# Four layers on one core: one copy per block end in layer 0, layer 1's norms in parts with its gates between the projections, and layer 2's norm in four parts

## The chip, the cores and the metric

The kernel runs on one core of one Trainium2 chip, in one launch. The metric is the device time of that core in microseconds (us); lower is better. A core has five engines with instruction queues of their own: PE (matrix products), ACT (activation functions, copies), DVE (elementwise work and statistics), POOL (elementwise work) and SP, which here only issues DMA transfers. Each takes its instructions in the order in which they were written into its queue, and waits where an operand isn't ready or a buffer isn't free.

## What is computed

The input `x` has the shape [2, 64, 64, 128] (batch, height, width, channels), all in fp32. Four layers are added to it in turn:

```python
x = x + L0_conv(_gn(x))      # attention over 4096 positions, 4 heads, relative-position bias
x = x + L1_conv(_gn(x))      # gated product, below
t = x as [2, 4096, 128]
t = t + L2_attn(_ln_t(t))    # causal, silu(scores**2), plus a positional product
t = t + L2_ffn(_ln_t(t))     # 64 experts, each takes its 8 best tokens
t = t + L3_attn(_ln_t(t))    # softmax attention over 4096 positions
t = t + L3_ffn(_ln_t(t))     # 8 experts, top 2 of a token
```

`_gn` is a group norm (32 groups), `_ln_t` a layer norm over the channels. The second layer, in which most of the change lies:

```python
xn = layer_norm(x, norm_a, norm_b)
left = (xn @ Wl + bl) * sigmoid(xn @ Wlg + blg)
right = (xn @ Wr + br) * sigmoid(xn @ Wrg + brg)
out_gate = sigmoid(xn @ Wog + bog)
out = einsum("bkjd,bkid->bijd", left, right) / n
out = layer_norm(out, on_a, on_b) * out_gate
return out @ Wo + bo
```

## The kernel before

`x` stays in SBUF as 64 rows of 128x128 (32 rows a batch; a "block" is four rows, 512 positions). Layers follow one another; where the text of one layer issues work of the next, it is interleaved by hand.

**Layer 0** (`l0_bounded`, L464). A unit is a batch, a pair of heads and a half of the queries: 8 units. Each has four query blocks of 512, and each block goes over 32 key tiles `k`: 1024 iterations and 32 block ends. An iteration makes scores (`sc`, PE, L588), exp (ACT, L596, into `es`), and a multiply by the bias `ew` (DVE, L597). `values()` (L538) runs two iterations behind: eight passes on PE (L546) add to the PSUM tile `o`, which has one buffer. With the last `k` of a block it copies `o` to `os`, half on ACT (L555), half on DVE (L556), since the value passes of the next block need `o`. `l0_finish` (L699) then adds the two halves (L705), transposes, divides and adds to `x`. Side work (the next unit's operands, statistics for layer 1, and layer 1's input norm for batch 0) is a list of generators, of which `piece()` and `more()` take steps in certain iterations.

**Layer 1** (`layer1`, L841). The input norm of batch 1 is `l1_rows` (L406): group norm of eight blocks on DVE (`group_norm`, two operations each, L157 and L158), statistics of all 32 rows (`row_stats`: bn_stats L165 and bn_aggr L166 for each row), one reciprocal root (`rstd`, L88: seven small steps with a square root on ACT and one Newton step), and then the norm of the rows, odd ones on ACT (L428), even ones on DVE (L169). `l1_turn` (L436) transposes a block on PE and scales it on ACT (L444). `gates(b, g)` makes the output gate's projection of a block: PE (L897) and ACT (L900) into `gate`; the gates of batch 0 stand before the norm, those of batch 1 between the turns. The projection loop goes over j = 0, 2, ... 62: two products of 128x512 into a PSUM tile, bias on DVE, sigmoid on ACT, two multiplies on POOL. Every fourth iteration takes the sigmoid of a part of `gate` (L947). The product stage makes `tri` (512 small products on PE, 16 ACT copies); the 16 additions of the bias `bo` to `x` (L974) are written there, but depend on nothing in it and were placed earlier in DVE's queue, between the steps of the norm of batch 1. The output norm goes over four groups of 16 columns: `stats`, then for each 4 columns the norm (three on ACT, one on DVE), transposes, an ACT step with the norm's scale and bias, and a multiply by the gate on POOL (for part of the last group on DVE, L995). `next(toeplitz)` issues the loading of layer 2's positional table (`l2_table`). Last, 16 blocks of `out @ Wo` are made on PE and added to `x` on DVE.

**Layer 2** (`layer2_attn`, L1083). Its parts are generators in a dictionary `jobs`, from which a planner takes steps between the iterations of the attention according to the steps left and the iterations left (`due`); `finish(key)` runs one to its end. `norm_stats(b)` (L1185) makes the statistics of all 32 rows of a batch and one reciprocal root; `keys(b, g)` needs them, normalizes block `g` (L169) and makes keys and values. Before the first iteration `norm_stats(0)`, `keys(0, 0)` and `prepare(0, 7, 0)`, the queries of the first block to be attended (block 7), are run to their end.

**Layer 3** (`l3_bounded`, L1935). Sixteen query blocks of 16 iterations each; `piece()` takes one step of a queue of jobs in each iteration, and two in the very first block. After the second to last block the routing of batch 1 and seven bias jobs (`f3_bias`, L1919: a transpose on PE, a copy on ACT, a product on PE, an addition on DVE) are queued; what isn't done when the last block ends is done after the loop. The experts follow.

## Time and profile before

| | us |
|---|---|
| median of three runs | 4883.54 (4882.14 to 4885.44) |
| the profiled execution | 4879.15 |
| its span in the profile | 4877.3 |

The profile shows one execution. Its stages, read from the timeline (us from the start of the span):

| stage | from | to |
|---|---|---|
| layer 0, loop | 120 | 2166 |
| layer 1, end of group norm of batch 1 | 2166 | 2182.7 |
| layer 1, norm of batch 1 and turns | 2182.7 | 2235.9 |
| layer 1, projection loop | 2235.9 | 2294.5 |
| layer 1, product | 2294.5 | 2312.3 |
| layer 1, output norm | 2312.3 | 2361.3 |
| layer 1, `out @ Wo` and additions to `x` | 2361.3 | 2378.1 |
| layer 2, up to the first scores | 2378.1 | 2397.8 |
| layer 2, attention and experts | 2397.8 | about 3780 |
| layer 3, attention | about 3780 | 4737 |
| layer 3, remaining bias jobs | 4737 | 4751 |
| layer 3, experts | 4751 | 4877 |

In the profile a group of instructions is named by its line, engine, operation, and the tile it writes, then (after `<-`) the tiles it reads. A time in brackets is how long the engine had been idle before an instruction, with what released it. PEclk is the share of full clock that PE was granted in a window. A window's row gives busy microseconds of each engine, with the count of its instructions.

### The profile page before, as it was taken

The page shows a single profiled execution, that of the slowest core. Times are in us where ns is not written, and L with a number is a line of the kernel's source. Part 1 is how long each engine was busy: PE and PEld are TensorE (multiplying, and loading weights), DVE is VectorE, ACT ScalarE, POOL GpSimd, SP SyncE. Part 2 cuts the span into 40 slices and gives each one's busy share as a digit, 9 for nine tenths or more (in the row PEclk, how much of TensorE's full clock was granted, in tenths as well). Part 3 has the DMA queues.
Part 4 walks back from the last instruction along what each step waited for, and adds up shares of the span by engine and source line. Part 5 has one row for each costly group of instructions (what it writes and reads, how often), then busy time and mean ns, then how long its engine had stood idle before and what let it go on. Part 6 is the DMA issues. An engine that isn't in the chain of part 4 may idle for free.

```text
span 4877.3 us, 78242 instructions
## 1 busy us (share of the span) xinstructions
PE 4514.3 (93%) x33260; PEld 1766.5 (36%) x33260; DVE 2943.3 (60%) x4845; ACT 2647.6 (54%) x3077; POOL 943.7 (19%) x848
## 2 busy tenths in 40 slices
PE   6999999999899999987789999999986999999999
PEld 4333333333233333335322223323224444444444
DVE  4676767676766767765755656555553544454447
ACT  3655555555556555554567666676740433333326
POOL 1000000000000000003355554655530100000008
PEclk7999999999999999998799999999987999999999
DMA  1000000000000000000000000000016000000001
GB/s 46 10 1 10 1 10 1 10 1 1 10 1 10 1 12 1 1 6 15 10 1 1 1 1 1 1 1 1 1 52 232 1 0 0 1 0 1 0 1 35
DMA packets 43210, 60.29 MB, mean 12 GB/s; under 512 B 4352, under 2 KB 25056, under 8 KB 41696
## 3 DMA queue, kind: packets, MB, share of 16 engines
q1 hardware_dynamic: 41552, 54.34, 3.6%
q8 instruction: 265, 4.34, 0.4%
q10 hardware_dynamic: 1296, 0.82, 0.1%
q14 instruction: 97, 0.79, 0.1%
HBM read 42.56 MB, written 4.19 MB: 10 GB/s over the span
## 4 chain that ended last, share of the span: by engine, by line
PE 37%; DVE 6%; ACT 3%; POOL 3%; issue 2%; DMA 0%; POOLq 0%; DVEq 0%; ACTq 0%
PE scl L2047 9%; PE oTl L2006 9%; PE l2sc L1422 5%; PE l2pos L1180 4%; PE l2av L1468 3%; PE f3ex L2156 2%; DVE l2es L1442 2%; POOL l2es L1445 2%; ACT l2es L1453 1%; ACT l2es L1433 1%; PE l2po L1388 1%; DVE l2a L169 0%; PE f3fpb L1930 0%; PE pol L1975 0%; PE l2pu L1180 0%
## 5 line engine op out<-in xcount | busy, mean ns | idle before, releaser
L597 DVE TENSOR_TENSOR l0es<-l0es,l0ew 128x1024 f32<-128x1024 f32 x1024 | 1252.0, 1227 | 601.5 <-ACT l0es L596 601.5
L596 ACT ACTIVATE l0es<-l0sc 128x1024 f32<-128x1024 f32 x1024 | 1042.7, 1023 | 722.5 <-PE l0sc L588 712.8
L546 PE MATMUL l0o<-l0es,l0v 64*33 64x512 f32 x8192 | 1070.0, 592 | 51.7 <-DVE l0os L556 46.4
L588 PE MATMUL l0sc<-l0qa,ka 64*64 64x512 f32 x8192 | 1081.9, 596 | 4.6 <-ACT l0es L596 4.6
L1453 ACT ACTIVATE l2es<-l2es 128x1024 f32<-128x1024 f32 (+3 forms) x576 | 559.3, 984 | 270.1 <-POOL l2es L1445 263.0
L1445 POOL TENSOR_TENSOR l2es<-l2es 128x1024 f32<-128x1024 f32 (+3 forms) x352 | 581.1, 1661 | 494.3 <-DVE l2es L1442 439.2
L2014 DVE TENSOR_TENSOR accl<-accl,esl 128x1024 f32<-128x1024 f32 x240 | 302.6, 1261 | 425.8 <-ACT esl L2058 422.4
L1442 DVE TENSOR_SCALAR l2es<-l2sc 128x1024 f32<-128x1024 f32 (+3 forms) x320 | 338.8, 1059 | 315.1 <-PE l2sc L1422 314.8
L2058 ACT ACTIVATE esl<-scl 128x1024 f32<-128x1024 f32 x240 | 245.5, 1023 | 481.7 <-PE scl L2047 456.6
L546 PEld LDWEIGHTS l0o<-l0es,l0v 64*33 64x33 f32 x8192 | 258.0, 108 | 659.3 <-issue 564.3
L588 PEld LDWEIGHTS l0sc<-l0qa,ka 64*64 64x64 f32 x8192 | 294.7, 133 | 546.8 <-issue 480.5
L2047 PE MATMUL scl<-l3qT,l3kT 128*128 128x512 f32 x1024 | 486.8, 595 | 0.0
L1422 PE MATMUL l2sc<-l2q,kept 32*128 32x512 f32 (+3 forms) x2304 | 389.4, 619 | 88.6 <-ACT l2es L1433 65.3
L2006 PE MATMUL oTl<-esl,l3v 128*128 128x512 f32 x960 | 450.9, 592 | 0.0
L722 POOL TENSOR_TENSOR x<-x,l0y 128x256 f32<-128x256 f32 x32 | 23.4, 732 | 2074.1 <-DVE l0y L717 1945.6
L1468 PE MATMUL l2av<-l2es,kept 128*32 128x512 f32 (+3 forms) x2304 | 310.6, 589 | 0.0
L1180 PE MATMUL l2pos<-kept 128*32 128x512 f32 x2416 | 297.0, 598 | 0.0
L2047 PEld LDWEIGHTS scl<-l3qT,l3kT 128*128 128x128 f32 x1024 | 188.5, 191 | 208.2 <-issue 192.5
L2006 PEld LDWEIGHTS oTl<-esl,l3v 128*128 128x128 f32 x960 | 181.8, 190 | 225.8 <-issue 221.5
L1433 ACT ACTIVATE l2es<-l2sc 128x1024 f32<-128x1024 f32 x224 | 226.1, 1009 | 53.9 <-PE l2sc L1422 52.5
L1422 PEld LDWEIGHTS l2sc<-l2q,kept 32*128 32x128 f32 x2304 | 115.9, 186 | 331.5 <-ACT l2es L1433 166.2
L1971 POOL TENSOR_TENSOR bothl<-accl 128x512 f32<-128x512 f32 x16 | 20.2, 1263 | 633.6 <-DVE accl L2014 633.6
(690 smaller groups left out, 3825.3 us busy)
## 6 DMA issues: line engine op xcount, KB each, us to landing
f2w<-in_L_ffn_weight_dram SPq DMA_DIRECT2D x32, 1024.0 KB, 13.4
l0ew<-l0ew SPq DMA_DIRECT2D x16, 512.0 KB, 5.1
x<-in_x_dram SPq DMA_DIRECT2D x8, 512.0 KB, 9.0
out_dram<-x SPq DMA_DIRECT2D x16, 256.0 KB, 2.3
kept<-in_L_attn_pos_rev_dram SPq DMA_DIRECT2D x1, 1792.0 KB, 6.7
ew<-in_L_ffn_expert_w_dram SPq DMA_DIRECT2D x1, 512.0 KB, 4.0
kept<-in_L_attn_pos_rev_dram SPq DMA_DIRECT2D x1, 256.0 KB
f2b<-in_L_ffn_weight_dram ACTq DMA_DIRECT2D x2, 128.0 KB, 2.5
```

The lines of the kernel that those rows point to most:

```text
L546: nc.tensor.matmul(o[64 * h : 64 * h + HD + 1, r, :], lhsT=v1[rows, k, 2 * pair + h, :], rhs=es[rows, h, :], start=(k == 0), stop=(k == NC ...
L588: nc.tensor.matmul(sc[64 * c : 64 * c + 64, h, :], lhsT=ka[rows, k0 : k0 + 64], rhs=qa[rows, k // (NC // 2), qs], start=True, stop=True,)
L596: nc.scalar.activation(es, sc, AF.Exp)
L597: nc.vector.tensor_tensor(es, es, ew[:, :, qs], ALU.mult)
L1180: nc.tensor.matmul(out[part], lhsT=lhsT[:, part], rhs=rhs, start=start, stop=stop)
L1422: nc.tensor.matmul(sc[:, h2, off:], lhsT=kT[hs, k * P : (k + 1) * P], rhs=q[hs, off:], start=True, stop=True,)
L1442: nc.vector.tensor_scalar(es[:, :, lo:], sc[:, :, lo:], root, None, ALU.mult)
L1445: nc.gpsimd.tensor_tensor(part, part, part, ALU.mult)
L1453: nc.scalar.activation(es[:, :, off:], es[:, :, off:], AF.Silu)
L1468: nc.tensor.matmul(avs[i][hs, off:], lhsT=v[:, k, hs], rhs=es[h // 2][:, h % 2, off:], start=(k == 0), stop=last,)
L2006: nc.tensor.matmul(oT, lhsT=vs[b][:, k, :], rhs=es[:, i, :], start=(k == 0), stop=(k == NC - 1),)
L2047: nc.tensor.matmul(sc[:, i, :], lhsT=kTs[b][:, k * P : (k + 1) * P], rhs=qT[:, qb * 512 : (qb + 1) * 512], start=True, stop=True,)
```

## The change

Layer 0: at a block's end ACT copies all of `o` in one instruction, and DVE copies nothing; in the text `values()` stands ahead of the multiply by the bias.

Layer 1, input norm of batch 1: in three parts (blocks 0 to 2, 3 to 5, 6 and 7). The statistics of a part are taken jointly: bn_stats of each row writes the count, mean and sum of squares of the row's even and odd elements, and five operations on all rows of the part at once form mean and variance from them, instead of a bn_aggr for each row. The rows of the first two parts are normalized on ACT, those of the third half on ACT and half on DVE. The gate projections move into the projection loop, one in every second iteration, with the sigmoid taken straight from PSUM. `bo` is loaded into a buffer of the product stage, so that its additions can't be placed before it. The output norm uses the same joint statistics, over groups of 8, 16, 16, 16 and 8 columns; the blocks of `out @ Wo` are taken in the order 0, 7, 1 to 6, 8 to 15.

Layer 2: `norm_stats` of batch 0 is made in four parts of two blocks, the first for blocks 0 and 7; the other three are jobs of the first iterations.

Layer 3: in the last block of batch 1 `piece()` is called twice in an iteration.

```diff
-    def rstd(self, out, var, eps, n, pool=None):
+    def rstd(self, out, var, eps, n, pool=None, scale=1.0):
...
-        nc.vector.tensor_scalar(v, var, eps, None, ALU.add)
+        if scale == 1.0:
+            nc.vector.tensor_scalar(v, var, eps, None, ALU.add)
+        else:
+            nc.vector.tensor_scalar(v, var, scale, eps, ALU.mult, ALU.add)
...
-                    nc.scalar.copy(os[rows, 0, :], o[rows, 0, :])
-                    nc.vector.tensor_copy(os[rows, 1, :], o[rows, 1, :])
+                    nc.scalar.copy(os[rows], o[rows])
...
-                        nc.vector.tensor_tensor(es, es, ew[:, :, qs], ALU.mult)
                         if len(waiting) == 2:
                             values()
+                        nc.vector.tensor_tensor(es, es, ew[:, :, qs], ALU.mult)
...
-            bo = self.load(wp, "bo", [P, C], row_bcast(ins["L1_conv_bo"], C))
 
             def stats(src, tag):
 
-                mv = sp.tile([P, GN, 2], F32, tag="mv", name=f"l1mv{tag}")
-                self.row_stats(mv, src, f"l1{tag}")
-                r = sp.tile([P, GN], F32, tag="r", name=f"l1r{tag}")
-                self.rstd(r, mv[:, :, 1], 1e-5, GN, sp)
-                m = sp.tile([P, GN], F32, tag="m", name=f"l1m{tag}")
-                nc.vector.scalar_tensor_tensor(m, mv[:, :, 0], -1.0, r, ALU.mult, ALU.mult)
-                return mv, r, m
+                n = src.shape[1]
+                st = sp.tile([P, 16, 6], F32, tag="st", name=f"l1st{tag}")
+                for i in range(n):
+                    nc.vector.bn_stats(st[:, i, :], src[:, i, :])
+                t = sp.tile([P, 3, 16], F32, tag="sum", name=f"l1sum{tag}")
+                mean, d, m2 = t[:, 0, :n], t[:, 1, :n], t[:, 2, :n]
+                nc.vector.tensor_tensor(d, st[:, :n, 1], st[:, :n, 4], ALU.subtract)
+                nc.vector.tensor_tensor(m2, st[:, :n, 2], st[:, :n, 5], ALU.add)
+                nc.vector.scalar_tensor_tensor(d, d, C / 4.0, d, ALU.mult, ALU.mult)
+                nc.vector.tensor_tensor(m2, m2, d, ALU.add)
+                r = sp.tile([P, 16], F32, tag="r", name=f"l1r{tag}")
+                self.rstd(r[:, :n], m2, 1e-5, n, sp, 1.0 / C)
+                nc.vector.tensor_tensor(mean, st[:, :n, 1], st[:, :n, 4], ALU.add)
+                m = sp.tile([P, 16], F32, tag="m", name=f"l1m{tag}")
+                nc.vector.scalar_tensor_tensor(m[:, :n], mean, -0.5, r[:, :n], ALU.mult, ALU.mult)
+                return r, m
...
-                rows = self.l1_rows(ps, xT[:, 1, :], 1, gst[:, 1], gb)
-                next(rows)
-                for g in range(NC // 4):
-                    gates(0, g)
-                for _ in rows:
-                    pass
-                for g in range(NC // 4):
-                    self.l1_turn(ps, xT[:, 1, :], 1, g, na, nb)
-                    gates(1, g)
+                self.group_rows(ps, gb, self.group_stats(ps, gst[:, 1], 1))
+
+                y = xT[:, 1, :].rearrange("p (n c) -> p n c", c=C)
+                for blocks in (range(3), range(3, 6), range(6, 8)):
+                    lo, hi = 4 * blocks[0], 4 * blocks[-1] + 4
+                    for g in blocks:
+                        self.group_norm(y[:, 4 * g : 4 * g + 4, :], 1, g, gb)
+                    given = stats(y[:, lo:hi, :], lo)
+                    for n in range(lo, hi):
+                        norm(y[:, n, :], n - lo, given, hi < NC or n % 2)
+                    for g in blocks:
+                        self.l1_turn(ps, xT[:, 1, :], 1, g, na, nb)
...
                 for j in range(0, S, 2):
+                    if j % 4 == 2:
+                        blk = slice((j // 4) * 512, (j // 4 + 1) * 512)
+                        pg = ps.tile([P, 512], F32, tag="pg", name=f"l1pg{j}", bufs=2)
+                        nc.tensor.matmul(
+                            pg, lhsT=wcat[:, 4 * C :], rhs=xnT[:, blk], start=True, stop=True
+                        )
+                        nc.scalar.activation(gate[:, blk], pg, AF.Sigmoid, bias=bog)
...
-                    if j % 8 == 6:
-                        part = gate[:, (j // 8) * 1024 : (j // 8 + 1) * 1024]
-                        nc.scalar.activation(part, part, AF.Sigmoid)
...
                 tri = xp.tile([P, S, C], F32, tag="xT", name="tri")
+                bo = up.tile([P, C], F32, tag="bo", name="bo", bufs=1)
+                nc.sync.dma_start(out=bo, in_=row_bcast(ins["L1_conv_bo"], C))
...
-                for g in range(S // GN):
-                    if g > 1:
+                at = 0
+                for g, n in enumerate((8, 16, 16, 16, 8)):
+                    if g in (2, 3):
                         next(toeplitz)
-                    given = stats(tri[:, GN * g : GN * (g + 1), :], f"o{g}")
+                    given = stats(tri[:, at : at + n, :], f"o{g}")
...
-                        eng = nc.vector if g == S // GN - 1 and lo % 8 else nc.gpsimd
+                        eng = nc.vector if j0 >= S - 16 and j0 % 8 else nc.gpsimd
...
-                for g in range(B * NC // 4):
+                for g in (0, 7, 1, 2, 3, 4, 5, 6, *range(8, 16)):
...
-            def norm_stats(b):
-                mv = self.small.tile([P, NC, 2], F32, tag="l2mv", name=f"l2mv{b}", bufs=2)
-                for n in range(NC):
-                    s6 = self.small.tile([P, 6], F32, tag="lst", name=f"l2st{b}_{n}")
-                    nc.vector.bn_stats(s6, self.x[:, b * NC + n, :])
-                    nc.vector.bn_aggr(mv[:, n, :], s6)
-                    if n % 4 == 3:
-                        yield 1
-                r = self.small.tile([P, NC], F32, tag="l2r", name=f"l2rs{b}", bufs=2)
-                self.rstd(r, mv[:, :, 1], 1e-5, NC)
-                stats[b] = mv, r
+            def norm_stats(b, lo, groups):
...
+                mv, r, where = stats[b]
+                hi = lo
+                for g in groups:
+                    where[g] = hi
+                    for n in range(4 * g, 4 * g + 4):
+                        s6 = self.small.tile([P, 6], F32, tag="lst", name=f"l2st{b}_{n}")
+                        nc.vector.bn_stats(s6, self.x[:, b * NC + n, :])
+                        nc.vector.bn_aggr(mv[:, hi, :], s6)
+                        hi += 1
+                    yield 1
+                pool = self.small if hi - lo == NC else wp
+                self.rstd(r[:, lo:hi], mv[:, lo:hi, 1], 1e-5, hi - lo, pool)
...
-                finish(("stats", b))
+                finish(("stats", b, 0 if b or g == 7 else (g + 1) // 2))
...
-            add(("stats", 0), 0, norm_stats(0))
+            parts = (0, 7), (1, 2), (3, 4), (5, 6)
+            add(("stats", 0, 0), 0, norm_stats(0, 0, parts[0]))
...
                 if i == 0:
+                    for part in range(1, 4):
+                        add(("stats", 0, part), 0, norm_stats(0, 8 * part, parts[part]))
...
-                        if b == 0 and qb == 0:
+                        if (b, qb) in ((0, 0), (B - 1, NB - 1)):
                             piece()
```

## The prediction

> **What bounds the kernel now.** I read the engine line of the page first, then the costliest groups, then PE's waits in layer 0 (120 to 2166 us), then the timeline of one block end there.
>
> ```profile
> PE 4514.3 (93%) x33260; PEld 1766.5 (36%) x33260; DVE 2943.3 (60%) x4845; ACT 2647.6 (54%) x3077; POOL 943.7 (19%) x848
> L546 PE MATMUL l0o<-l0es,l0v 64*33 64x512 f32 x8192 | 1070.0, 592 | 51.7 <-DVE l0os L556 46.4
> PE l0o L546 <- DVE l0os L556: 46.4, 30, 3.8
> ```
>
> PE is the bound: 93% of the span. What is to be had is PE's idle time and the stages where it is idle. The last line (engine, waited for, total, times, longest) gives the largest wait: 30 of the 32 block ends hold PE, 46.4 us in all. I split these by the timeline: 22 are ordinary ends of 1.29, 7 are ends of a unit of about 2.03, and one, near 1236 us, is 3.8; that makes 46.4. An ordinary end (start, duration, what it waited for in brackets):
>
> ```profile
> 2110.02 1.04 PE L588 MATMUL l0sc<-l0qa,ka 64*64 64x512 f32 x8
> 2110.34 0.58 ACT L555 COPY l0os<-l0o 97x512 f32<-97x512 f32 x1
> 2110.46 1.23 DVE L597 TENSOR_TENSOR l0es<-l0es,l0ew 128x1024 f32<-128x1024 f32 x1 [0.49 <-ACT l0es L596]
> 2111.12 1.02 ACT L596 ACTIVATE l0es<-l0sc 128x1024 f32<-128x1024 f32 x1 [0.19 <-PE l0sc L588]
> 2111.60 0.68 DVE L556 COPY l0os<-l0o 97x512 f32<-97x512 f32 x1
> 2112.34 1.06 PE L546 MATMUL l0o<-l0es,l0v 64*33 64x512 f32 x8 [1.29 <-DVE l0os L556]
> ```
>
> ACT copies its half at once; DVE's half stands behind a 1.23 us multiply, and the one PSUM tile `o` stays taken until 2112.28. The windows of layer 1 and of the start of layer 2 (window, length, busy us and instruction count of PE, PEld, DVE, ACT, POOL, then PE's clock, DMA share, GB/s):
>
> ```profile
> 2182.70:2207.90 25.20, 8.69 (x16) 3.40 (x14) 25.12 (x99) 11.83 (x16) 0.00 (x0) 0.64 0.00 1
> 2207.90:2235.90 28.00, 14.39 (x49) 7.46 (x50) 7.38 (x21) 20.34 (x35) 0.00 (x0) 0.83 0.00 1
> 2235.90:2294.50 58.60, 55.06 (x129) 37.46 (x127) 39.20 (x32) 21.92 (x34) 45.72 (x64) 1.00 0.00 0
> 2320.30:2361.30 41.00, 25.92 (x80) 13.69 (x80) 28.33 (x123) 30.85 (x67) 21.45 (x16) 0.62 0.06 15
> 2378.10:2397.80 19.70, 11.18 (x55) 4.56 (x55) 12.96 (x63) 3.73 (x6) 1.26 (x1) 0.65 0.00 1
> ```
>
> Norm of batch 1: first DVE is full, then ACT. Projection loop: PE is full. Output norm: nobody is full, ACT leads. Start of layer 2: a chain of waits.
>
> **Layer 0, one copy.** Removed: 32 DVE copies. ACT's copy grows from 97x512 (0.58) to 97x1024; no such row exists. Ends: twice 0.58 = 1.16, and 0.90 if half of the small one were fixed cost; I take 1.02, the exp row on 128x1024. Then `o` is free at 2110.34 + 1.02 + 0.06 (the gap seen between 2112.28 and 2112.34) = 2111.42 instead of 2112.34: 0.92 gained. The tile of the next value passes was multiplied before 2110, and the next (2110.46) ends at 2111.69, before the second group needs it. ACT's next exp goes from 2111.12 to about 2111.4, but the multiply after it gains the 0.68 of the gone copy, so nothing new is late. At a unit's end (copy at 437.61, PE at 439.98) it is 1.29. Sum: 22 x 0.92 = 20.2; 7 x 1.29 = 9.0; the 3.8 wait keeps some 0.4 to 0.8, so 3; the very last end 0.3. **-32.5**, range -25 to -37. Moving `values()` ahead of the multiply changes the order on no engine.
>
> **Layer 1, norm of batch 1.** DVE before the first part's shift `m`: 12 adds and multiplies of blocks 0 to 5 at 0.605 = 7.3, 15 statistics at 0.22 = 3.3, 12 small operations at 0.1 = 1.2: `m` at 2182.7 + 11.8 = 2194.5 (before: 2207.39). From there ACT is the bound: 28 norms at 0.39 = 10.9 and 8 turns at 0.77 = 6.2, with some 3 of waits: the projections can start at 2214.6 instead of 2235.9, **-21.3**. The bias adds of `bo` (L974), which stood between the steps of the reciprocal root (5.7 us from 2201.89 to 2207.57), are gone from here.
>
> **The gates move into the projection loop.** That loop has 55.06 of 58.6 busy on PE with 128 passes of 0.43. Sixteen fp32 gates of two passes add 32 x 0.43 = **+13.7**, hidden by nothing. On ACT the 16 sigmoids from PSUM (about 0.69 each, 11 us) replace 9 us of wider ones: it has 37 us free; POOL's 45.7 also fits. At 2182 PE's gate passes came 0.86 apart until 2186.9 and then 0.43: 4.5 us after idleness at half rate cost 2.3. The new loop starts after a thinner stretch: **+2**. Together -21.3 + 13.7 + 2 = **-5.6**, range -9 to -2.
>
> **`bo` loaded late, its 16 adds in the product.** The DMA keeps its place in SP's order, now waiting for the loop's end; behind it stand only loads for the next stage. The other row broadcasts land in 3.0 to 4.8 us; 16 adds at 0.6 = 9.7; DVE is idle in the 17.8 us of the product. **0**; if the load lands after 8 us, the first statistics of the output norm wait by the rest, 1 us or so.
>
> **Output norm, groups 8, 16, 16, 16, 8.** The first group has 8 rows less of statistics (8 x 0.26 = 2.1), of which the next group's 9 queued ones ahead of the reciprocal take 0.5 back: first ACT norm -1.6. ACT's 30.85 of work stays, its gaps are about 10 us. Five chains of 13 small DVE operations replace four of 7. Against it stands a rule.
>
> ```profile
> 2319.82 0.14 DVE L102 TENSOR_TENSOR l1ro<-rs_r,rs_q 128x16 f32<-128x16 f32 x1
> ...
> 2329.23 1.47 POOL L995 TENSOR_TENSOR kept<-l1yn,l1gate 128x512 f32<-128x512 f32 x1 [1.02 <-ACT l1yn L993]
> 2329.31 1.42 DVE L102 TENSOR_TENSOR l1ro<-rs_r,rs_q 128x16 f32<-128x16 f32 x1
> ```
>
> The same operation takes 0.14 and, beside a POOL multiply, 1.42. The Trainium skill, "SBUF — State Buffer", section "Who interferes with whom", says that a DVE operation with two SBUF inputs and a GpSimd one exclude each other entirely. By the rule every two-input step that meets POOL's 21.45 of 41 us is held: half of 5 x 9 such steps, 22 x 1.1 = 25 us on DVE, and this part would end some +4. By the rows only 4 of 28 small steps were held, 1.1 longer on average. With 65 at that rate 9 are held, 5 more = 5.5, mostly off ACT's path since the next group's chain runs a group ahead: I put 1.5 on the path, the earlier start -1.6, fewer ACT gaps from the last short group -2: **-2**, range -7 to +4. The x adds after it are bound by PE (15.94 of 16.8): 0.
>
> **Start of layer 2 in four parts.** Of the chain that ended the wait:
>
> ```profile
> 2382.88 0.18 DVE L93 TENSOR_SCALAR rs_v<-l2mv 128x32 f32<-128x32 f32 x1
> 2384.64 1.11 DVE L169 TENSOR_SCALAR l2xn_0k<-x,l2mv,l2rs 128x128 f32<-128x128 f32 x4
> ```
>
> Blocks 0 and 7 now have their root before the last x add ends at 2378.1, so the first norm is there: -6.5. Given back: 24 rows of statistics (24 x 0.26 = 6.2) and three chains of 7 come in the first iterations, where DVE has gaps of some 6 us: about +1. ACT now alternates between Sqrt and Silu there: six more table loads.
>
> ```profile
> 2220.18 0.77 ACT L444 ACTIVATE xT<-l1pt,nb,na 128x512 f32<-128x512 f32 x1
> 2220.96 1.28 ACT L947 ACT_TABLE_LOAD   x1
> 2222.26 1.06 ACT L947 ACTIVATE l1gate<-l1gate 128x1024 f32<-128x1024 f32 x1
> ```
>
> A load takes 1.28 with no gap on either side. The Trainium skill, "ScalarE: Activation LUTs", "What ACT_TABLE_LOAD costs", adds a drain of about 1.38 us. Six cost 7.7 by the row, 16 by the rule, with which this part would end at +6; I take the row. The first is partly in idle time, the rest delays squares and silus of the first blocks (40.30 busy of 52.2 after 2397.8): +3.5. Sum **-2**, range -6.5 to +5.
>
> **Layer 3, last block, two pieces per iteration.** Four bias pairs leave the tail, where one takes 1.65 (4 x 1.65 = 6.6), and enter the PE-bound loop at 0.11 + 0.86 = 0.97 each (+3.9), with one wait of about 0.3: **-2.5**, range -4 to -1.
>
> **Sum**: -32.5 - 5.6 - 2 - 2 - 2.5 = -44.6. The profiled execution took 4879.15 (span 4877.3, 1.9 around it), so 4834.5. It lies 4.4 below the median of the runs shown; against that median: **4839**.
>
> **Rivals.** (A) *The wait changes its name*: the long ACT copy delays the exps and PE waits for them; half of layer 0's gain is lost, +16: **4855**. For it: ACT's copy now takes 1.02 of a period of 1.72. Against: PE has two score tiles, and only 4.6 us of waits for exp in the whole layer. (B) *The parts close the gaps*: in the output norm and in layer 2's start ACT runs without pauses, -11 more: **4828**. For it: ACT's 10 us of gaps there. (C) *Slower: the projection loop stays at half rate.* PE is thin before it (clock 0.64 in the norm), and if its clock doesn't rise, 160 passes take 0.86: +69 against the forecast, **4908**. It decides once 2/3 of the loop (46 us of loss) run cold. Against: clock 1.00 in the loop of before, and 4.5 us sufficed at 2186. (D) *Layer 1 and 2 give nothing*, the loads and held operations eat all: +9.6, **4849**.
>
> **Chances.** Forecast 0.54, A 0.14, B 0.16, C 0.03, D 0.13. Range 4821 to 4857: from B less 7 to A; the extremes of the unknown costs seldom meet. A difference of 0.2% (9.8 us) is about what a measurement tells from no change: faster 0.95, same 0.02, slower 0.03.
>
> **What would show it.** PE's wait for `os` near 15 us and named after ACT; layer 0 ends 32 earlier; projections start 32 + 21 earlier and last 72 to 75; `bo`'s adds end before the product; first norm of layer 2 directly after the last x add, with Sqrt loads among the silus; three bias pairs in the tail. Wrong if ACT's copy exceeds 1.3, if waits for exp rise above 20 us, or if layer 2's first scores come no earlier relative to the last x add.

## The result and the profile after

| | before | changed |
|---|---|---|
| median of four runs, us | 4882.84 (4881.95 to 4885.44) | 4828.86 (4826.12 to 4829.54) |
| profiled execution: span, us | 4877.3 | 4824.3 |

The ratio is 0.9888, with a 95% interval of 0.987 to 0.9905: the change makes the kernel 54 us (1.1%) faster. The forecast was 4839, its range 4821 to 4857. The range held the time; the single value was 10 us too slow. First the page of the changed kernel and PE's waits in its layer 0 loop (engine, what it waited for, total, times, longest):

```profile
PE 4514.4 (94%) x33260; PEld 1761.8 (37%) x33260; DVE 2918.7 (61%) x4784; ACT 2661.0 (55%) x3091; POOL 945.1 (20%) x848
...
L549 PE MATMUL l0o<-l0es,l0v 64*33 64x512 f32 x8192 | 1068.0, 591 | 19.8 <-ACT l0os L558 12.5
```

```profile
PE l0o L549 <- ACT l0os L558: 12.5, 29, 0.7
PE l0o L549 <- DVE l0es L601: 7.0, 11, 1.6
PE l0sc L590 <- ACT l0es L598: 4.7, 6, 2.3
```

PE's busy time is what it was (4514): the change takes away waiting, not work. The largest wait fell from 46.4 to 12.5 us and is now for ACT's copy; the waits for exp (4.6 before, 4.7 now) did not grow, those for the multiply went from 5.1 to 7.0. An ordinary block end of the changed kernel, from its timeline (start, duration, in brackets the wait; PE's weight loads left out):

```profile
2074.07 1.04 PE L590 MATMUL l0sc<-l0qa,ka 64*64 64x512 f32 x8
...
2074.39 1.01 ACT L558 COPY l0os<-l0o 97x1024 f32<-97x1024 f32 x1
2074.51 1.23 DVE L601 TENSOR_TENSOR l0es<-l0es,l0ew 128x1024 f32<-128x1024 f32 x1 [0.49 <-ACT l0es L598]
2075.30 1.03 ACT L598 ACTIVATE l0es<-l0sc 128x1024 f32<-128x1024 f32 x1
...
2075.46 1.06 PE L549 MATMUL l0o<-l0es,l0v 64*33 64x512 f32 x8 [0.35 <-ACT l0os L558]
```

The copy of 97x1024 took 1.01 us, and PE waited 0.35 where it had waited 1.29. The windows of layer 1 and of layer 2's start (length, then busy us of PE, PEld, DVE, ACT, POOL, then PE's clock, DMA share, GB/s):

```profile
2143.00:2154.90 11.90, 0.00 (x0) 0.00 (x0) 11.79 (x44) 0.75 (x3) 0.00 (x0) 0.50 0.00 0
2154.90:2172.50 17.60, 11.09 (x33) 5.67 (x33) 8.84 (x47) 16.14 (x37) 0.00 (x0) 0.50 0.00 1
2172.50:2246.40 73.90, 70.34 (x160) 43.95 (x160) 39.18 (x32) 30.64 (x49) 45.61 (x64) 0.98 0.01 1
2262.90:2315.30 52.40, 26.66 (x88) 13.72 (x84) 34.45 (x153) 34.38 (x72) 21.30 (x16) 0.67 0.14 47
2331.20:2341.90 10.70, 8.08 (x58) 3.40 (x56) 10.56 (x50) 4.27 (x6) 1.27 (x1) 1.00 0.01 2
```

The norm of batch 1 is now 29.5 us of two kinds: first DVE is full and PE and ACT are idle, then ACT is full (16.14 of 17.6). The projection loop is still PE's, and longer. The additions of `bo` (2246.74 to 2256.46) lie inside the product and cost nothing there, as forecast. The last row is the stretch up to layer 2's first scores: 10.7 us at full clock, where the kernel before had 19.7 at 0.65.

Set beside each other by stage (first and last starts in the two profiles), the 53 us are:

| stage | before | changed | difference | in the sum of the prediction |
|---|---|---|---|---|
| start to the first score of layer 0 | 97.3 | 95.2 | -2.1 | 0 |
| layer 0 loop, to the last value pass | 2069.0 | 2034.2 | -34.8 | -32.2 |
| to the group norm's row copy | 16.0 | 13.2 | -2.8 | -0.3 |
| norm of batch 1, to the first projection | 53.6 | 29.9 | -23.7 | -21.3 |
| projection loop, to the product | 58.6 | 73.9 | +15.3 | +15.7 |
| product and output norm, to `out @ Wo` | 66.9 | 68.9 | +2.0 | -2 |
| `out @ Wo` | 15.5 | 15.8 | +0.3 | 0 |
| layer 2, to its last value pass | 1231.6 | 1225.1 | -6.5 | -2 |
| to layer 3's first score | 174.4 | 174.2 | -0.2 | 0 |
| layer 3 loop | 952.6 | 956.9 | +4.3 | +4.2 |
| bias tail, to the experts | 17.2 | 10.8 | -6.4 | -6.6 |
| experts | 124.6 | 126.3 | +1.7 | 0 |

One execution differs from another in stages whose text is the same: the start takes 95.1 to 97.8 us over all profiles, the experts 124.6 to 126.8, the product 14.9 to 17.5 (at a granted clock of 1.00 to 0.83), the loop with all its gates 73.9 to 75.5, and the old norm of batch 1 53.6 in the kernel before and 56.4 in run 1 below. So what follows compares stages first, with this scatter in mind, and whole times second.

### The profile page after: what moved, and what is told of

Same layout as the page of the kernel before. It is cut to its first block, busy times and chain, and to the rows that moved or that the text cites. A ratio compares the mean times of both kernels' runs of the same rounds, so it can differ in the third digit from the quotient of the medians.

```text
span 4824.3 us, 78221 instructions
## 1 busy us (share of the span) xinstructions
PE 4514.4 (94%) x33260; PEld 1761.8 (37%) x33260; DVE 2918.7 (61%) x4784; ACT 2661.0 (55%) x3091; POOL 945.1 (20%) x848
## 4 chain that ended last, share of the span: by engine, by line
PE 78%; DVE 9%; ACT 6%; POOL 3%; issue 2%; DMA 1%; SPq 0%; DVEq 0%; ACTq 0%; POOLq 0%
PE l0sc L590 17%; PE l0o L549 16%; PE scl L2076 9%; PE oTl L2035 9%; PE l2sc L1448 5%; PE l2pos L1195 5%; PE l2av L1494 3%; DVE l2es L1468 2%; PE f3ex L2185 2%; POOL l2es L1471 2%; PE l0pw L643 1%; ACT l2es L1479 1%; ACT l0es L598 1%; PE l1p L938 1%; ACT l2es L1459 1%
## 5 line engine op out<-in xcount | busy, mean ns | idle before, releaser
L549 PE MATMUL l0o<-l0es,l0v 64*33 64x512 f32 x8192 | 1068.0, 591 | 19.8 <-ACT l0os L558 12.5
L1195 PEld LDWEIGHTS l2pos<-kept 128*32 128x32 f32 x2416 | 78.4, 111 | 175.1 <-issue 174.3
```

The source lines that it names most:

```text
L549: nc.tensor.matmul(o[64 * h : 64 * h + HD + 1, r, :], lhsT=v1[rows, k, 2 * pair + h, :], rhs=es[rows, h, :], start=(k == 0), stop=(k == NC ...
L1195: nc.tensor.matmul(out[part], lhsT=lhsT[:, part], rhs=rhs, start=start, stop=stop)
```

## Experiments

The runs were made in three groups, each on one chip; their ratios are to runs of the kernel before on the same chip (medians 4880.85, 4879.8 and 4878.85). The changed kernel was 54.0 us below the kernel before in the first measurement and 47.7 in the last group, so whole times of different groups do not settle a few microseconds.

### 1. The copy alone

```diff
--- before
-                    nc.scalar.copy(os[rows, 0, :], o[rows, 0, :])
-                    nc.vector.tensor_copy(os[rows, 1, :], o[rows, 1, :])
+                    nc.scalar.copy(os[rows], o[rows])
```

> The kernel before with the one ACT copy at a block's end and nothing else. Theory: the wait for DVE's half is most of what the change gains, and it is gained in layer 0 alone; in the two profiles layer 0's loop went from 2069.0 to 2034.2 us, so this kernel is 35 us faster than before (ratio 0.993), its PE waits for the copy fall from 46.4 to about 12.5 us, and a further 3 us come from the clock: the 3.8 us wait near 1236 us, after which passes ran at half rate for some 6 us, is shorter and is no longer followed by so many slow passes. Rival: the gain in layer 0 needs the multiply behind the value passes in the text too, then the waits stay above 25 us and the gain is below 25. Second rival: no clock effect, then the gain is 31 to 32.

Measured: 4845.81 us, ratio 0.9926 (0.9909 to 0.9942), 35 us faster. The loop took 2032.4 us, 36.6 less than before. The waits were 12.6 for the copy, 7.7 for the multiply, 4.7 for exp, together 31.1 less. So two thirds of the whole gain is this one line, and the place of `values()` in the text adds nothing. The clock had its part, but not where I looked for it. This is the long wait of the kernel before (PE only, eight passes a row):

```profile
1231.13 1.98 PE L588 MATMUL l0sc<-l0qa,ka 64*64 64x512 f32 x8 [2.30 <-ACT l0es L596]
1236.90 1.93 PE L546 MATMUL l0o<-l0es,l0v 64*33 64x512 f32 x8 [3.79 <-DVE l0os L556]
1238.61 1.93 PE L588 MATMUL l0sc<-l0qa,ka 64*64 64x512 f32 x8
...
1241.68 1.03 PE L588 MATMUL l0sc<-l0qa,ka 64*64 64x512 f32 x8
```

Eight passes take 1.93 after the waits and 1.03 some 5 us later. In this run the wait of 3.79 is gone, but the one of 2.30 remains and some four groups still run slow after it. What went are slow passes elsewhere. Six units end in a wait of 2.03 us in the kernel before; after two of them, near 193 and 1760 us, PE ran at half rate for some 3 us. First the kernel before, with a window's row (the clock is third from its end), then this run at the same unit's end:

```profile
192.96 1.52 PE L546 MATMUL l0o<-l0es,l0v 64*33 64x512 f32 x8 [2.03 <-DVE l0os L556]
194.24 1.95 PE L588 MATMUL l0sc<-l0qa,ka 64*64 64x512 f32 x8
193.00:196.50 3.50, 3.50 (x20) 1.04 (x24) 1.76 (x2) 0.25 (x1) 0.00 (x0) 0.56 0.00 0
```

```profile
191.50 1.06 PE L546 MATMUL l0o<-l0es,l0v 64*33 64x512 f32 x8 [0.73 <-ACT l0os L555]
192.38 1.04 PE L587 MATMUL l0sc<-l0qa,ka 64*64 64x512 f32 x8
```

The wait is 0.73 now, and nothing slow follows it at any of the six. Over the loop 87 passes of scores and values are slow before, 56 in the changed kernel and 39 in this run. A slow pass costs 0.11 us more (eight of them start 1.71 us apart for 0.86), so this estimate makes 3.3 and 5.1 us; PE's busy time in the loop fell by 3.0 and 5.6. The second rival (no clock effect) is out. The 56 and the 39 differ although the waits of these two kernels hardly do.

### 2. Layer 2's norm in one part, and PE kept busy

```diff
--- changed
-            parts = (0, 7), (1, 2), (3, 4), (5, 6)
+            parts = (tuple(range(NB)),)
...
-                    for part in range(1, 4):
+                    for part in range(1, 1):
...
-                finish(("stats", b, 0 if b or g == 7 else (g + 1) // 2))
+                finish(("stats", b, 0))
```

> The changed kernel with layer 2's norm of batch 0 in one part, as before (the order of the output blocks stays 0, 7, 1 to 6). Theory: the parts gain 6.6 net, so this is about 6 us slower than the changed kernel (4835), the first norm of layer 2 comes 7 us after the last addition to x instead of 1, the six extra table loads are gone, and PE's passes up to the first scores run at half rate again (keys' product 1.94 us instead of 1.07). Rival (the sum of the prediction): the parts gain 2 only, and the rest is noise of one execution; then it is at most 3 us slower.

The second run adds idle products ahead of layer 2:

```diff
+            warm = ps.tile([P, 512], F32, tag="misc", name="l2warm")
+            for n in range(40):
+                nc.tensor.matmul(
+                    warm[:, :P], lhsT=self.ident, rhs=self.ident, start=True, stop=True
+                )
             for key in list(jobs):
                 finish(key)
```

> The same as the run with one part, but PE makes 40 idle 128x128 products (their result is not used) between the last output block and layer 2's first transposes, so it isn't idle while the norm's chain runs. Theory: of the 10.1 us that the changed kernel gained up to the first scores, 3.4 are not waiting but clock: the 6.8 us of idleness halve PE's rate for the passes after it. Then this run has the same late first norm as the run with one part, its keys' product takes about 1.07 instead of 1.94, and it is about 3 us faster than the run with one part. Rival: the slower passes come from something else in that stretch (waits for ACT, weight loads); then they stay at 1.94 and the time is the same within 1 us.

Measured: 4832.91 with one part, 4828.57 with the idle products. PE in the first of them, and then in the second:

```profile
2342.82 1.15 PE L1232 MATMUL l2t_0k<-ident,l2xn_0k 128*128 128x128 f32 x4 [7.61 <-DVE l2xn_0k L172]
2344.86 1.94 PE L1195 MATMUL l2pk<-l2xT_0k,wk 128*32 128x512 f32 x8 [0.89 <-DVE l2xT_0k L1234]
```

```profile
2337.08 9.20 PE L1515 MATMUL l2warm<-ident 128*128 128x128 f32 x80 [0.30 <-ACT gwT L84]
2346.11 0.60 PE L1232 MATMUL l2t_0k<-ident,l2xn_0k 128*128 128x128 f32 x4
2347.49 1.07 PE L1195 MATMUL l2pk<-l2xT_0k,wk 128*32 128x512 f32 x8 [0.78 <-DVE l2xT_0k L1234]
```

After 7.61 us of idleness the keys' product takes 1.94 us, after idle work 1.07. From the first transposes to the first scores it is 13.0 in the first run and 8.9 in the second: the second price of the wait is 4.1 us. (The 40 products, two passes each, were too many: they held the transposes up by some 1.7 us.) Counted from the last output block, the second run's first scores come 2.4 us earlier, and with swings between it is still 2.5 us ahead after 1440 of the layer's 2304 score passes. Up to the last value pass, however, the two take 1229.1 and 1228.8 us. The lead goes just after, where PE was longer at half rate in this execution; the first run, then the second:

```profile
3140.00:3150.00 10.00, 9.18 (x60) 3.78 (x61) 5.03 (x10) 3.83 (x4) 4.40 (x4) 0.90 0.01 2
3140.00:3150.00 10.00, 10.00 (x52) 5.29 (x44) 3.51 (x7) 3.67 (x4) 3.48 (x3) 0.66 0.00 0
```

So the gain in passes is shown. One in the whole time isn't, beyond the difference of two medians; whether the idle products cause the later half rate is open.

The parts are worth 1229.1 - 1225.1 = 4.0 us by these two profiles: the first scores come 10.4 us earlier, 6.4 are given back later. But the attention from its first scores on, with one part, took 1208.0 us in this execution, 1210.1 with the idle products, 1210.9 in the kernel before and 1211.7 in run 1. With this scatter the parts are worth 4 to 7 us, and my theory's 6.6 is neither shown nor refuted; the rival's 2 lies below this. The whole time does not decide it: the run with one part is 47.9 us below the kernel before, the changed kernel 54.0 and 47.7.

### 3. The output norm

```diff
--- changed
-                for g, n in enumerate((8, 16, 16, 16, 8)):
+                for g, n in enumerate((16, 16, 16, 16)):
```

> The changed kernel with the output norm in four groups of 16 columns, as before, but with the joint statistics. Theory: the new grouping costs 3.9 us after its first norm, because a first group of 8 columns gives ACT only 5 us of work while the next 16 columns' statistics are made, and the square root of the last group stands behind ACT's norms; with four groups the stage is 2 to 4 us shorter than in the changed kernel and the whole 4826. Rival: the loss is in the longer chains of small DVE operations beside POOL's multiplies, then four groups help by 1 us at most, or the first norm comes 1.8 us later and nothing is regained (4830).

Measured: 4827.46 us; from the product's end to `out @ Wo` 50.2 us against 52.4 in the changed kernel (52.3 and 52.4 in the two runs of experiment 2). The first norm starts 1.7 us later, and the stage is still 2.2 shorter; the joint statistics alone are about as fast as the old ones (50.4 before, 49.8 in the two other runs with the old norm). So the new grouping loses what it was meant to give. Its place, ACT in the changed kernel and then DVE, with POOL, at the same time:

```profile
2285.71 0.78 ACT L1006 ACTIVATE l1yn<-l1yt,onb,ona 128x512 f32<-128x512 f32 x1 [0.29 <-PE l1yt L1004]
2289.89 0.21 ACT L98 ACTIVATE rs_s<-rs_v 128x16 f32<-128x16 f32 x1 [3.40 <-DVE rs_v L96]
2290.17 1.65 ACT L896 ACTIVATE tri<-tri,l1mo,l1ro 128x128 f32<-128x128 f32 x4
```

```profile
2285.39 2.95 POOL L1008 TENSOR_TENSOR kept<-l1yn,l1gate 128x512 f32<-128x512 f32 x2 [0.70 <-ACT l1yn L1006]
2286.31 0.63 DVE L882 TENSOR_TENSOR l1sumo<-l1sto 128x16 f32<-128x16 f32 x1
2286.87 0.68 DVE L1073 COPY kept<-l2flip 128x512 f32<-128x512 f32 x1
2287.47 0.91 DVE L102 TENSOR_TENSOR rs_q<-rs_r 128x16 f32<-128x16 f32 x1
```

ACT waits 3.4 us at the root of the fourth group, because DVE reaches its variance late; the third group's norms stand behind it, and their own shift was ready only at 2290.13 too. Copies for layer 2's table stand between DVE's steps, and two small ones take 0.63 and 0.91 instead of 0.16: they end as a POOL multiply ends (the second at 2288.38, POOL at 2288.34). With four groups the roots of the second and third are taken one after the other, long before the third group's norms, which begin at 2289.46:

```profile
2276.97 0.31 ACT L98 ACTIVATE rs_s<-rs_v 128x16 f32<-128x16 f32 x2
```

Can the waits be had back with the new groups, by issuing the statistics earlier?

```diff
--- changed
+                coming = stats(tri[:, :8, :], "o0")
...
-                    given = stats(tri[:, at : at + n, :], f"o{g}")
+                    given = coming
                     for lo in range(0, n, 4):
+                        if lo == n // 2 and g < 4:
+                            coming = stats(
+                                tri[:, at + n : at + n + sizes[g + 1], :], f"o{g + 1}"
+                            )
```

> The changed kernel, but in the output norm the statistics of the next group are issued halfway through the group before it, ahead of its second half's norms. Groups stay 8, 16, 16, 16, 8. Theory: the stage of 52.4 us from the product's end is long because ACT waits at each group's start for a shift that DVE finishes late (2.15, 3.4 and some 2.5 us seen), and because the square root stands behind the norms of the group before; issued earlier these go, and the stage takes 47 to 50 us, the whole 2 to 5 us less than the changed kernel. Rival: DVE's own order (the copies for layer 2's table, small steps held beside POOL's multiplies) sets the shifts; then the stage stays above 51.

Measured: 4830.84 us, the stage 52.9. A miss: ACT's waits for a late shift shrank from 2.4 to 1.3 us in sum and those for a variance from 4.9 to 4.6, but its waits for transposes grew from 6.3 to 8.7. The rival's number holds; that DVE's order is the reason fits the rows above, and was not tried by itself.

### 4. The gates

Batch 0's gates ahead of the norm of batch 1, where PE is idle:

```diff
--- changed
+                for g in range(NC // 4):
+                    gates(0, g)
                 y = xT[:, 1, :].rearrange("p (n c) -> p n c", c=C)
...
-                    if j % 4 == 2:
-                        blk = slice((j // 4) * 512, (j // 4 + 1) * 512)
+                    if j % 8 == 6:
+                        blk = slice(L + (j // 8) * 512, L + (j // 8 + 1) * 512)
```

> The changed kernel, but the eight output gates of batch 0 are made before the norm of batch 1 (product on PE, sigmoid from PSUM on ACT), where in the changed kernel's profile PE is idle for 11.9 us and ACT works 0.75 of them; the eight of batch 1 stay in the projection loop, one in four iterations. Theory: in the loop a gate costs its two passes on PE, 0.86 us, hidden by nothing, so the loop gets 8 x 0.86 = 6.9 us shorter (67.0 instead of 73.9), and two table loads before the norm (2 x 1.28) delay the first square root by at most 1.5: 5 to 7 us faster than the changed kernel, about 4823. Rival: the loop is not bound by PE's passes but by POOL's two multiplies of 0.71 each and the buffers, then it gets less than 3 us shorter. Second rival: the gates run at half rate ahead of the norm, push the norm's first square root and the turns back by 5 us or more, and nothing is left.

All gates out of the loop (`gates(1, g)` again behind each turn, the loop's block removed):

```diff
--- the run above
                         self.l1_turn(ps, xT[:, 1, :], 1, g, na, nb)
+                        gates(1, g)
...
-                        nc.scalar.activation(gate[:, blk], pg, AF.Sigmoid, bias=bog)
+                    if j % 16 == 14:
+                        part = gate[:, L + (j // 16) * 1024 : L + (j // 16 + 1) * 1024]
+                        nc.scalar.activation(part, part, AF.Sigmoid)
```

> The changed kernel with all gates out of the projection loop: batch 0's ahead of the norm of batch 1, batch 1's between the turns as before (ACT adds the bias, the sigmoids in place follow where ACT takes them). Theory: the loop loses all 15.3 us that it gained, but the stage of the norm, whose second half ACT sets (16.1 busy of 17.6 us), takes 8 x 0.6 + 4 x 0.96 + 1.3 = 10 us more ACT work, and PE's turns stand behind gates that wait for ACT; it starts the loop 10 to 14 us later: 1 to 5 us faster than the changed kernel, and not faster than the run with only batch 0's gates ahead of the norm. Rival: the gates are hidden in the norm entirely (as one would say of work that PE does while idle); then it is 12 us faster or more. Second rival: the coupling costs more than 15 us, and the moving of the gates was a gain in itself.

Measured: 4822.57 and 4826.36 us. The second half of the norm and the loop, first in the run with batch 0's gates early, then in the run with all outside:

```profile
2157.80:2176.10 18.30, 11.12 (x33) 5.71 (x33) 9.41 (x51) 16.63 (x39) 0.00 (x0) 0.50 0.01 1
2176.10:2243.80 67.70, 64.16 (x144) 40.91 (x144) 39.19 (x32) 25.98 (x41) 45.71 (x64) 0.97 0.00 1
```

```profile
2154.50:2186.30 31.80, 18.92 (x48) 9.20 (x49) 8.82 (x46) 25.42 (x49) 0.00 (x0) 0.68 0.00 1
2186.30:2245.00 58.70, 55.13 (x131) 37.51 (x129) 39.19 (x32) 21.92 (x34) 45.79 (x64) 0.99 0.00 1
```

From the row copy to the product:

| | norm | loop | sum |
|---|---|---|---|
| before | 53.6 | 58.6 | 112.2 |
| changed | 29.9 | 73.9 | 103.8 |
| all gates outside | 44.2 | 58.7 | 102.9 |
| batch 0's outside | 30.7 | 67.7 | 98.4 |

(In seven other profiles with the changed kernel's text the sum is 104.6 to 105.4, the loop being longer.) The moving of the gates is worth nothing in itself: with all of them outside, the two stages take 0.9 less than in the changed kernel, up to 2.5 less than in its other profiles. What pays is to see that the two batches differ. Batch 0's gates fit into the stretch where PE and ACT are idle: they add 0.8 us to the norm and take 6.2 off the loop, which gives 5.4. Batch 1's add 13.5 between the turns and take 9.0 off the loop: moving them into the loop was right, by 4.5. The two nearly cancel.

### 5. The late `bo` alone

```diff
--- before
-            bo = self.load(wp, "bo", [P, C], row_bcast(ins["L1_conv_bo"], C))
...
                 tri = xp.tile([P, S, C], F32, tag="xT", name="tri")
+                bo = up.tile([P, C], F32, tag="bo", name="bo", bufs=1)
+                nc.sync.dma_start(out=bo, in_=row_bcast(ins["L1_conv_bo"], C))
```

> The kernel before with the bias of layer 1's output loaded in the product stage, and nothing else: its 16 additions can't stand between the steps of the reciprocal root. Theory: of the 21 to 24 us that the norm of batch 1 got shorter, the additions are 5 (root and shift ready at 2202.4 instead of 2207.4), the parts the rest; from the group norm's row copy to the first projection 48 to 49 us instead of 53.6, the additions hidden in the product stage, the whole 5 us faster than before. Rival: the additions only filled DVE's waits for ACT, then less than 2 us; second rival: they cost in the product stage what they gave in the norm, then the whole is the same.

Measured: 4876.05 us, ratio 0.9986 (0.9979 to 0.9993), so 3 to 10 us faster. From the row copy to the first projection it is 51.6 us, 2.0 less than in the profile of before, not 5. The first norm on ACT did come 4.7 us earlier (20.6 us after the row copy instead of 25.3), and the product stage stayed at 16.5. The rest went behind it, on PE:

```profile
2213.84 2.08 PE L896 MATMUL l1pg<-xT,wcat 128*128 128x512 f32 x2 [0.92 <-ACT xT L444]
...
2217.68 2.08 PE L896 MATMUL l1pg<-xT,wcat 128*128 128x512 f32 x2 [0.92 <-ACT xT L444]
...
2225.28 1.12 PE L896 MATMUL l1pg<-xT,wcat 128*128 128x512 f32 x2 [0.87 <-ACT xT L444]
```

The gates take 2.08 us up to the one at 2221.5 and 1.12 after it; with a slow gate the cycle of turn and gate takes up to 3.84 us instead of 2.57. In the kernel before only the first gate was that slow. But run 1, whose layer 1 has the text of the kernel before, additions included, has four slow gates as well. The kernel before, then run 1:

```profile
2214.58 2.08 PE L897 MATMUL l1pg<-xT,wcat 128*128 128x512 f32 x2 [5.52 <-ACT xT L444]
...
2218.43 1.12 PE L897 MATMUL l1pg<-xT,wcat 128*128 128x512 f32 x2 [0.92 <-ACT xT L444]
```

```profile
2179.07 2.07 PE L896 MATMUL l1pg<-xT,wcat 128*128 128x512 f32 x2 [0.92 <-ACT xT L444]
...
2190.51 1.12 PE L896 MATMUL l1pg<-xT,wcat 128*128 128x512 f32 x2 [0.87 <-ACT xT L444]
```

There the first norm came 25.3 us after the row copy, and the stage took 56.4 us. Against it the late `bo` gives 4.8, the whole of what its first norm won. So the theory's 5 us fits, both rivals are out, and the slow gates need no earlier start. Why one execution has one of them and another four is open.

### 6. Layer 2 in two parts, layer 3, and a combination

```diff
--- changed
-            parts = (0, 7), (1, 2), (3, 4), (5, 6)
+            parts = (0, 7), (1, 2, 3, 4, 5, 6)
```

> The changed kernel with layer 2's norm of batch 0 in two parts instead of four: blocks 0 and 7, then the other six. Theory: the first scores come as early as in the changed kernel (10.8 us after the last output block), and of six table loads in the first iterations two remain, so 4 x 1.28 = 5.1 us of ACT work go; but the second part must have all 24 rows' statistics (6.2 us of DVE) before block 1's keys: from the last output block to the last value pass 1223 to 1226 us instead of 1225.0, the whole within 2 us of the changed kernel. Rival: a table load costs its 1.28 and a drain of about 1.38 beside it, as the rule has it, and ACT bounds the first iterations; then four loads less bring 8 to 10 us.

Measured: 4822.1 us; first scores 10.6 us after the last output block, last value pass 1221.9 against 1225.1 (1225.3 to 1226.2 in the other profiles with four parts). Four table loads and two roots less bring 3 us net, 2.6 of them within the first 480 of 2304 score passes, and the loads look like this in the changed kernel:

```profile
2342.31 0.21 ACT L98 ACTIVATE rs_s<-rs_v 128x8 f32<-128x8 f32 x1
2343.03 1.02 ACT L1459 ACTIVATE l2es<-l2sc 128x1024 f32<-128x1024 f32 x1 [0.51 <-PE l2sc L1448]
2344.07 1.28 ACT L1479 ACT_TABLE_LOAD   x1
2345.37 1.06 ACT L1479 ACTIVATE l2es<-l2es 128x1024 f32<-128x1024 f32 x1
```

1.28 us, with 0.02 on either side.

Layer 3 with one piece per iteration in its last block again:

```diff
--- changed
-                        if (b, qb) in ((0, 0), (B - 1, NB - 1)):
+                        if b == 0 and qb == 0:
```

> The changed kernel with one piece per iteration in layer 3's last block, as before. Theory: seven bias jobs stand in the tail again (from the last value pass to the experts' first product 17.2 us instead of 10.8) and layer 3's loop is 4.3 us shorter (948.8 instead of 953 from its first score to its last value pass); 2 to 3 us slower than the changed kernel. Rival: the loop's 4.3 us came from something else (scatter of executions), then the loop stays and the run is 6 us slower.

Measured: 4832.93 against 4831.13 for the changed kernel in the same group. From the first to the last score the loop took 949.5 us, where the changed kernel took 953.7 in both its profiles, and the tail, from the last value pass to the experts' first product, 17.4 instead of 10.5 and 10.3. The edit gives and takes as priced, 2 to 3 us net.

The changed kernel again, and a kernel with batch 0's gates early, four groups in the output norm and two parts in layer 2 (the three edits shown above, together):

> The changed kernel itself, as the measure for the others of this group on the same chip: 4826 to 4830, ratio 0.989.

> The changed kernel with three edits that the earlier runs single out: batch 0's gates ahead of the norm of batch 1 (norm and loop together 98.4 instead of 103.8 us), the output norm in four groups of 16 (50.2 instead of 52.4), layer 2's norm in two parts (3.1 less up to the last value pass). Theory: they lie in three stages that follow one another and add: 5.4 + 2.2 + 3.1 = 10.7 us faster than the changed kernel, about 4818. Rival: a stage takes over what another gives (later loads of layer 2's table, a colder PE), then it gains less than 7.

Measured: 4831.13 (4827.55 to 4831.49), ratio 0.9895, and 4816.96 us (4815.54 to 4817.22), ratio 0.9867 (0.9849 to 0.9885). The combination is faster than both kernels, by 14 us than the changed one in the same group, by 12 than its first median. Against the changed kernel's first profile the stages account for 10 of this: norm and loop 97.8 (103.8), output norm 50.9 (52.4), layer 2 1222.7 (1225.1). Against its second they account for 12, since its loop was 1.6 us longer.

## Why the prediction was right, and where it was off

**Layer 0.** The step held: copy 1.01 us for an assumed 1.02, the waits 46.4 to 12.5 (I had said about 15), the listed waits of PE together 31.9 less for a sum of 32.5, no new wait for exp. Rival A (the gain halves) is out. I had miscounted the ends: 23 are ordinary and 6 end a unit, which makes 0.3 less. Some 3 us more came from slow passes that no longer follow the waits (experiment 1), which the sum had not.

**Norm of batch 1.** The size held (-23.7 for -21.3). The first norm came 11.75 us after the row copy, for 12.2 reckoned, and ACT's part took 18.1 for 20.1. The run with all gates outside divides the gain: its norm takes 44.2 us, so 14.3 are the gates that left the stage and 9.4 the parts, the joint statistics and `bo`. Of these only `bo` was measured apart: 4.7 on DVE, and alone 2.0 against the kernel before or 4.8 against run 1.

**Loop.** 73.9 for 58.6 + 13.7 + 2 = 74.3, and 74.7 to 75.5 in seven other profiles: gates of PE's time, hidden by nothing, and a cold start. Rival C (half rate throughout) is out; the first four projection passes ran slow (3.39 us for four, 3.60 for eight later). What the prediction did not ask is what the gates cost where they stood. Experiment 4 shows it: for batch 1 more than in the loop, for batch 0 next to nothing, and in sum about the same.

**Output norm.** Here a term failed: "fewer ACT gaps from the last short group -2". The first norm came 2.1 earlier for 1.6, and then ACT's gaps grew, from 10.2 to 13.6 us: +2.0 for -2. A short first group shortens the time in which DVE may prepare the second and third; this reading is argued from the rows, while the run with four groups (experiment 3) shows that the loss is the grouping's. The other term, held steps, was counted too high. A chain has 12 steps on DVE, so 60 stand there and not 65; five of them were stretched, to between 0.46 and 1.25 us, where I had reckoned with 9. The rule of the Trainium skill ("SBUF — State Buffer", "Who interferes with whom") agrees with the rows. By it a DVE step with two SBUF inputs and a step of GpSimd (here POOL) that reads SBUF keep each other out. Of the 45 small two-input steps, the four that began inside a POOL multiply with 0.4 us or more of it left all ended within 0.04 us of its end. Only five more touched a multiply, at its first or last 0.15 us. The fifth stretched step has one input and ended the same way (2276.15, the multiply at 2276.12). So the +4 that I drew from the rule came from my estimate of 22 meetings, not from the rule.

**Start of layer 2.** -6.5 for -2. The first norm came 6.7 us earlier for 6.5 forecast, and 3.6 us were given back later for 4.5. What was missing is the second price of the wait: at half rate the products up to the first scores took 12.7 us, and now 9.3. The windows of before showed it (0.65 of the clock), and I read it only as "a chain of waits". Of the 8.4 us between the sum (-44.6) and the spans (-53.0) this stage is the largest term, 4.5. That the passes are slower after the wait is shown by the two runs of experiment 2. How much of the 4.5 is due to it is not, since the attention behind it varies by up to 3.7 us between executions with the norm in one part.

**Table loads.** The row was right, and the rule of the Trainium skill ("ScalarE: Activation LUTs", "What ACT_TABLE_LOAD costs") too dear here: 1.28 without a drain at its sides, and four loads less gave 3 us net where it would make 10.6.

**Layer 3.** -2.1 in loop and tail (+4.3, -6.4) for -2.5, with three bias pairs left in the tail as forecast.

The upper end of the range, 4857, lies 2 above rival A, which it was said to be. Rival B gave nearly the time that was measured (4828 for 4828.86), but by a mechanism that did not occur: ACT's gaps in the output norm grew. That B came closer than the forecast is chance. The remaining 2.1 us of the start and 2.8 less 0.3 ahead of the norm lie in unchanged work. The start scatters by as much. The other is a statistic that DVE began some 2.4 us late, with no cause that the profile shows, in both kernels with two copies (before and `bo` late), and without that delay in runs 1 and 2 and the changed kernel; it is open.

## What to carry to other kernels

A PSUM tile with one buffer is free when the slowest of its readers is done: look at what stands in the queue ahead of each reader, and give the whole tile to the engine that comes to it first, if the longer instruction still fits its period. Before work is moved out of a stage, ask which engine bounds each half of that stage: eight gates fitted where PE and ACT were idle, the other eight cost 13.5 us there and 9.0 in the loop. And before a few microseconds are given a cause, look at the same stage in a second kernel that shares its text: the slow gates looked like the work of the late `bo` until run 1 showed them too. A smaller first group starts a pipeline sooner, but it also shortens the cover under which the next group is made ready.

## What the hardware showed beyond what was expected

Idleness of PE can be paid twice. After 7.6 us without work a product of 8 passes took 1.94 us and after idle work 1.07. A wait of 2.03 us in layer 0 was followed by some 3 us at a clock of 0.56 and 0.57 in two cases of six, one of 0.73 us in none of six. In the norm of batch 1 the granted clock was still 0.50 in the second half, although PE was busy for 11.1 of 17.6 us there. And how long the half rate lasts is not fixed by the kernel's text: the same product stage took 14.9, 16.5 or 17.5 us at a mean clock of 1.00, 0.90 or about 0.84, and the same gates ran slow once in one execution and four times in another.
